# A recurrent scorer on one core: fp32 instructions of 50 rows for the item-0 correction, and a shorter setup

## Chip, cores and metric

One core of a Trainium2 chip. The metric is the device time of one execution in microseconds (us). Numbers of timed runs are medians of several executions. "Span" is the length of the profiled execution on the core, some 2 us less than the time of the same execution.

## The reference, cut to what matters

```python
emb = emb_table.at[0].set(0.0)              # item 0 counts as a row of zeros
e = emb[seq]                                # 1024 x 50 x 128
prefix = jnp.cumsum(e, axis=1)
uF = prefix / minimum(t + 1, lengths)       # running mean
y  = (uF - uF.mean(0)) * rsqrt(uF.var(0) + 1e-5) * gamma + beta
# scan over the 50 steps: v = v + (x - v)/2; spike = v >= 1; v = v - spike
scores = spikes.mean(over the steps) @ emb.T   # 1024 x 100001, fp32
```

The kernel gathers from the table as it lies in memory, where row 0 is not zero. So wherever the index is 0, row 0 has to be taken off again. That correction is what the change alters.

## The kernel before

Stage one runs through the 50 time steps. GpSimd gathers 1024 rows per step (eight gathers of 128 rows), TensorE transposes them into an accumulator `pre` in PSUM that runs through all steps, VectorE and ScalarE compute the running mean, the normalisation and the spikes, and TensorE counts the spikes. Stage two multiplies the counts with the table and writes 410 MB of scores.

```python
# gathers: three row buffers ("gather", bufs=3), tag "e"
def gather(t):
    es[t] = gp.tile([P, B], F32, tag="e")
    for n in range(NB):                      # NB = 8
        nc.gpsimd.indirect_dma_start(out=es[t][:, n*P:(n+1)*P], in_=table,
                                     in_offset=IndirectOffsetOnAxis(ap=idx[:, n, t:t+1]))
gather(0)
make_identity(nc, ident)
# ...
# the mask of zero indices, twice (rows 0..49 and 64..113), transposed to zT, 128 x 1024
isz = gp.tile([P, NB, P], F32, tag="e")
nc.vector.memset(isz, 0.0)
for u in (0, P // 2):
    nc.vector.tensor_single_scalar(isz[:, :, u:u+T], idx, 0.0, ALU.is_equal)
# ... eight transposes, then
nc.vector.tensor_copy(zT, zps)               # zT is float32r
# row 0 split into a rounded part (upper rows) and the rest (lower rows): r0n
rlen = once.tile([P, B], F32)
nc.vector.tensor_copy(rlen, len_i)           # 128 x 1024
nc.vector.reciprocal(rlen, rlen)             # 128 x 1024

def row0(t):                                 # ScalarE: row 0 into the rows t and 64 + t
    nc.scalar.activation(l, r0n, AF.Copy, scale=sel[:, t:t+1])
def correct(t, l):                           # TensorE: one float32r pass for each half of the batch
    for h in range(2):
        nc.tensor.matmul(pre[h], lhsT=l, rhs=zT[:, h*BANK:(h+1)*BANK], start=t == 0, stop=False)

# a time step t
gather(t + 1)                                # cut: the place of this call
# transposes of step t into pre[h]; uF = max(rlen, 1/(t+1)) * pre[h]; bn_stats
correct(t + 1, l)
# normalisation on VectorE and ScalarE; spikes; then
counted(t - 1, s, h)                         # TensorE, behind the correction
```

## Time and profile before

| | before |
|---|---|
| time, 3 runs | 1645.34 us (1644.9 to 1645.82) |
| profiled span | 1721.3 us |
| stage one, until the first output matmul | 593.4 us in the profile |
| gathers | 400 on GpSimd, 0.947 us each and 0.30 us between them |
| correction | 100 matmuls, 72.7 us in all |
| first uF | at 28.66 us |

How to read the profile. The busy tenths cut the span into 40 slices, one digit a slice. A group line gives engine, operation, tiles and number, then busy us, mean ns of one, and the engine's idle time ahead of it with what ended it. "issue" as a releaser is time in which the engine waited for nothing that the profile shows, and "remote" one for which it found no releaser. A timeline row is start, duration, engine, line, tiles, and in brackets the idle time before it. POOL is GpSimd, PE is TensorE, DVE is VectorE, ACT is ScalarE. The lines are in the prediction.

Note that the profiled execution took 1723.2 us, 78 us longer than the timed ones.

### The profile page before, as it was taken

The page shows a single profiled execution, that of the slowest core. Times are in us where ns is not written, and L with a number is a line of the kernel's source. Part 1 is how long each engine was busy: PE and PEld are TensorE (multiplying, and loading weights), DVE is VectorE, ACT ScalarE, POOL GpSimd, SP SyncE. Part 2 cuts the span into 40 slices and gives each one's busy share as a digit, 9 for nine tenths or more (in the row PEclk, how much of TensorE's full clock was granted, in tenths as well). Part 3 has the DMA queues.
Part 4 walks back from the last instruction along what each step waited for, and adds up shares of the span by engine and source line. Part 5 has one row for each costly group of instructions (what it writes and reads, how often), then busy time and mean ns, then how long its engine had stood idle before and what let it go on. Part 6 is the DMA issues. An engine that isn't in the chain of part 4 may idle for free.

```text
span 1721.3 us, 13874 instructions
## 1 busy us (share of the span) xinstructions
PE 1141.8 (66%) x4526; PEld 820.3 (48%) x4526; DVE 969.4 (56%) x1261; ACT 636.3 (37%) x698; POOL 379.5 (22%) x406
## 2 busy tenths in 40 slices
PE   2233333433344478877788777877778888888886
PEld 1112222221222356655566555666556666666664
DVE  5557756765667645554455444554445555555554
ACT  1222222221223344443444434444334444444443
POOL 7666666666666000000000000000000000000000
PEclk9855555555555599999999999998998899999999
DMA  9811111111111199999999999999999999999998
GB/s 267 234 44 48 48 48 44 48 49 46 45 49 46 38 391 397 401 400 393 388 394 402 394 391 393 395 400 390 396 396 390 403 410 414 402 405 406 403 402 349
DMA packets 98004, 488.75 MB, mean 284 GB/s; under 512 B 14827, under 2 KB 16652, under 8 KB 48780
## 3 DMA queue, kind: packets, MB, share of 16 engines
q1 hardware_dynamic: 85132, 461.63, 68.9%
q0 software_dynamic: 12800, 26.24, 5.3%
q8 instruction: 35, 0.57, 0.1%
q14 instruction: 37, 0.30, 0.0%
HBM read 78.21 MB, written 409.60 MB: 283 GB/s over the span
## 4 chain that ended last, share of the span: by engine, by line
DMA 48%; DVE 23%; PE 10%; another core or an unknown queue 9%; ACT 5%; issue 4%; POOL 0%; ACTq 0%; DVEq 0%; SPq 0%
DMA scores<-o 48%; PE po L301 9%; DVE bs L229 4%; ACT o L311 4%; DVE uF L228 4%; DVE v L267 3%; DVE s L199 3%; DVE negv L266 2%; DVE o L309 2%; ACT v L264 1%; DVE mv L233 1%; DVE a L257 1%; DVE r L255 1%; DVE q L254 0%
## 5 line engine op out<-in xcount | busy, mean ns | idle before, releaser
L301 PE MATMUL po<-hi,countR 128*128 128x512 f32 x1568 | 679.9, 434 | 179.5 <-ACT o L311 176.4
L309 DVE TENSOR_SCALAR o<-po 128x1024 f32<-128x1024 f32 x392 | 478.9, 1222 | 460.3 <-DMA scores<-o 428.3
L301 PE MATMUL po<-lo,countR 128*128 128x512 f32 x1568 | 645.0, 412 | 0.0
L311 ACT ACTIVATE o<-po 128x1024 f32<-128x1024 f32 (+1 forms) x392 | 399.9, 1020 | 633.2 <-DMA scores<-o 506.0
L301 PEld LDWEIGHTS po<-hi,countR 128*128 128x128 f32 x1568 | 316.0, 202 | 330.5 <-ACT o L311 243.0
L122 POOL DMA_INDIRECT e<-in_L_rec_emb_table,idx x400 | 378.8, 947 | 184.7 <-issue 109.3
L301 PEld LDWEIGHTS po<-lo,countR 128*128 128x128 f32 x1568 | 316.4, 202 | 60.1
L179 PE MATMUL pre<-zT,l 128*128 128x512 f32 x100 | 72.7, 729 | 264.4 <-DVE uF L228 196.0
L179 PEld LDWEIGHTS pre<-zT,l 128*128 128x128 f32 x100 | 27.0, 271 | 306.0 <-issue 192.2
L92 DVE TENSOR_TENSOR lo<-pt,hi 128x1024 fp32r<-128x1024 f32 x98 | 119.7, 1221 | 87.9 <-ACT hi L91 86.2
L228 DVE SCALAR_TENSOR_TENSOR uF<-rlen,pre 128x512 f32<-128x512 f32 x100 | 67.9, 679 | 144.8 <-remote 129.3
L237 ACT ACTIVATE r<-mv,eps 128x1 f32<-128x1 f32 x50 | 14.7, 295 | 351.4 <-DVE mv L233 307.2
L90 PE MATMUL pt<-ident,rows 128*128 128x128 f32 x782 | 108.4, 283 | 19.3 <-ACT o L311 12.0
L90 PEld LDWEIGHTS pt<-ident,rows 128*128 128x128 f32 x782 | 89.2, 144 | 52.4 <-ACT o L311 38.2
L189 PE MATMUL count<-s,ident_h 128*128 128x512 bf16 x100 | 50.7, 608 | 88.9 <-DVE s L199 67.8
L91 ACT CAST hi<-pt 128x1024 fp32r<-128x1024 f32 x98 | 98.5, 1005 | 16.1 <-remote 11.3
L219 PEld LDWEIGHTS pre<-ident,e 128*128 128x128 f32 x400 | 86.7, 228 | 21.3 <-issue 18.6
L219 PE MATMUL pre<-ident,e 128*128 128x128 f32 x400 | 95.4, 418 | 0.0
L264 ACT ACTIVATE v<-uF,hgb,a 128x1024 f32<-128x1024 f32 (+1 forms) x51 | 60.8, 1192 | 52.0 <-DVE r L255 16.2
L229 DVE BATCH_NORM_STATS2 bs<-uF 128x6 f32<-128x512 f32 x100 | 69.4, 694 | 3.4
L267 DVE SCALAR_TENSOR_TENSOR v<-negv,v 128x1024 f32<-128x1024 f32 (+1 forms) x51 | 61.6, 1209 | 15.6 <-issue 7.3
L189 PEld LDWEIGHTS <-ident_h 128*128 128x128 bf16 x100 | 12.2, 122 | 103.2 <-issue 102.9
(41 smaller groups left out, 286.3 us busy)
## 6 DMA issues: line engine op xcount, KB each, us to landing
scores<-o SPq DMA_DIRECT2D x384, 1024.0 KB
scores<-o SPq DMA_DIRECT2D x8, 848.5 KB
e<-in_L_rec_emb_table,idx POOLq DMA_INDIRECT x400
rows<-in_L_rec_emb_table SPq DMA_DIRECT2D x1, 832.0 KB
rows<-in_L_rec_emb_table SPq DMA_DIRECT2D x48, 0.5 KB
len_i<-in_r_lengths SPq DMA_DIRECT2D x1, 512.0 KB
idx<-in_r_seq SPq DMA_DIRECT2D x1, 200.0 KB
r<-in_L_rec_emb_table SPq DMA_DIRECT2D x1, 64.0 KB
```

The lines of the kernel that those rows point to most:

```text
L90: nc.tensor.transpose(pt[:, k0 : k0 + kw], r[:kw, (h0 + k0) // P, :], ident[:kw, :kw])
L91: nc.scalar.copy(hi[:, :hw], pt[:, :hw])
L92: nc.vector.tensor_tensor(lo[:, :hw], pt[:, :hw], hi[:, :hw].bitcast(F32), ALU.subtract)
L122: nc.gpsimd.indirect_dma_start(out=es[t][:, n * P : (n + 1) * P], out_offset=None, in_=table, in_offset=bass.IndirectOffsetOnAxis(ap=idx[: ...
L179: nc.tensor.matmul(pre[h], lhsT=l, rhs=zT[:, h * BANK : (h + 1) * BANK], start=t == 0, stop=False, skip_group_check=True,)
L219: nc.tensor.matmul(pre[h][:, k : k + P], lhsT=e[:, h * BANK + k : h * BANK + k + P], rhs=ident, start=False, stop=last, is_transpose=True, ...
L228: nc.vector.scalar_tensor_tensor(uF[:, cs], rlen[:, cs], 1.0 / (t + 1), pre[h], ALU.max, ALU.mult)
L229: nc.vector.bn_stats(bs[:, h, :], uF[:, cs])
L267: nc.vector.scalar_tensor_tensor(vt[:, cs], negv[:, cs], -0.5, vt[:, cs], ALU.mult, ALU.add)
L301: nc.tensor.matmul(po[:, k0 : k0 + kw], lhsT=countR[:, n * P : (n + 1) * P], rhs=part[:, k0 : k0 + kw], start=j == 0, stop=j == 1,)
L309: nc.vector.tensor_scalar_mul(o[:, h0 : h0 + hw], po[:, :hw], 1.0 / T)
L311: nc.scalar.mul(o[:, h0 : h0 + hw], po[:, :hw], 1.0 / T)
```

## The change

The intent is an exact and simpler correction: one true fp32 product of 50 rows (one per time step) in place of the split into two float32r parts in 100 of 128 rows; and a setup that takes reciprocals of 128x8 lengths instead of a 128x1024 broadcast. "Four instructions" in the short description are, as I read it, the four that the hardware profile records for a step: two for each of the two matmuls.

```diff
-        len_i = up.tile([P, B], I32, tag="uF", name="len_i")
-        nc.sync.dma_start(out=len_i, in_=lengths...to_broadcast([P, B]))
-        r0 = once.tile([P, D], F32, tag="r0", name="r0")
+        len_i = once.tile([P, NB], I32, tag="len_i", name="len_i")
+        nc.sync.dma_start(out=len_i, in_=lengths.rearrange("(n p) -> p n", p=P))
+        r0 = once.tile([T, D], F32, tag="r0", name="r0")
 ...
+        make_identity(nc, ident)
         gather(0)
-        make_identity(nc, ident)
 ...
-        isz = gp.tile([P, NB, P], F32, tag="e", name="isz")
-        nc.vector.memset(isz, 0.0)
-        for u in (0, P // 2):
-            nc.vector.tensor_single_scalar(isz[:, :, u : u + T], idx, 0.0, ALU.is_equal)
+        isz = gp.tile([P, NB, T], F32, tag="e", name="isz")
+        nc.vector.tensor_single_scalar(isz..., idx..., 0.0, ALU.is_equal)
 ...
-        zT = once.tile([P, B], F32R, tag="zT", name="zT")
-        nc.vector.tensor_copy(zT, zps)
-        (row 0 split in two parts, and the selector sel)
+        zT = once.tile([T, B], F32, tag="zT", name="zT")
+        nc.scalar.copy(zT, zps[:T, :])
+        r0n = once.tile([T, D], F32, tag="r0n", name="r0n")
+        nc.vector.tensor_scalar_mul(r0n, r0, -1.0)
+        rl = once.tile([P, NB], F32, tag="rl", name="rl")
+        nc.vector.tensor_copy(rl, len_i)
+        nc.vector.reciprocal(rl, rl)
+        rb = gp.tile([P, NB, P], F32, tag="e", name="rb")
+        nc.vector.tensor_copy(rb, rl.unsqueeze(2).to_broadcast([P, NB, P]))
+        (eight transposes of rb into rps)
-        nc.vector.tensor_copy(rlen, len_i)
-        nc.vector.reciprocal(rlen, rlen)
+        nc.vector.tensor_copy(rlen, rps)
 ...
-            l = sp.tile([P, D], F32R, tag="l", name=f"l_{t}")
-            nc.scalar.activation(l, r0n, AF.Copy, scale=sel[:, t : t + 1])
+            l = sp.tile([T, D], F32, tag="l", name=f"l_{t}")
+            nc.scalar.activation(l, r0n, AF.Copy, scale=ident[:T, t : t + 1])
```

More of the change, by code (lines that the diff above doesn't have):

```diff
@@ L44, in rec_kernel @@
     NB = B // P
-    assert D == P and B == HALF and T <= P // 2
+    assert D == P and B == HALF and T <= P
     ctx.enter_context(tc.manual_schedule())
@@ L106, in rec_kernel @@
         nc.sync.dma_start(out=idx, in_=seq.rearrange("(n p) t -> p n t", p=P))
-        len_i = up.tile([P, B], I32, tag="uF", name="len_i")
-        nc.sync.dma_start(out=len_i, in_=lengths.rearrange("(o b) -> o b", o=1).to_broadcast([P, B]))
-        r0 = once.tile([P, D], F32, tag="r0", name="r0")
-        nc.sync.dma_start(out=r0, in_=table[0:1, :].to_broadcast([P, D]))
+        len_i = once.tile([P, NB], I32, tag="len_i", name="len_i")
+        nc.sync.dma_start(out=len_i, in_=lengths.rearrange("(n p) -> p n", p=P))
+        r0 = once.tile([T, D], F32, tag="r0", name="r0")
+        nc.sync.dma_start(out=r0, in_=table[0:1, :].to_broadcast([T, D]))
         gb = once.tile([P, 2], F32, tag="gb", name="gb")
@@ L141, in rec_kernel @@
+        nc.vector.tensor_single_scalar(
+            isz.rearrange("p n t -> p (n t)"), idx.rearrange("p n t -> p (n t)"), 0.0, ALU.is_equal
+        )
         zps = vp.tile([P, B], F32, tag="v1", name="zps")
         for n in range(NB):
-            nc.tensor.transpose(zps[:, n * P : (n + 1) * P], isz[:, n, :], ident)
-        zT = once.tile([P, B], F32R, tag="zT", name="zT")
-        nc.vector.tensor_copy(zT, zps)
-        r0hi = once.tile([P, D], F32R, tag="r0hi", name="r0hi")
-        nc.scalar.copy(r0hi, r0)
@@ L148, in rec_kernel @@
-        r0n = once.tile([P, D], F32, tag="r0n", name="r0n")
-        nc.vector.tensor_scalar_mul(r0n, r0hi.bitcast(F32), -1.0)
-        up2 = slice(P // 2, P)
-        nc.vector.tensor_tensor(r0n[up2, :], r0hi[up2, :].bitcast(F32), r0[up2, :], ALU.subtract)
-        sel = once.tile([P, P // 2], F32, tag="sel", name="sel")
-        nc.vector.tensor_tensor(sel, ident[:, : P // 2], ident[:, P // 2 :], ALU.add)
+            nc.tensor.transpose(zps[:T, n * P : (n + 1) * P], isz[:, n, :], ident)
+        zT = once.tile([T, B], F32, tag="zT", name="zT")
@@ new lines, in rec_kernel @@
+        nc.scalar.copy(zT, zps[:T, :])
[6 more added lines that the diff above has]
+        nc.vector.tensor_copy(rb, rl.unsqueeze(2).to_broadcast([P, NB, P]))
+        rps = vp.tile([P, B], F32, tag="v0", name="rps")
+        for n in range(NB):
+            nc.tensor.transpose(rps[:, n * P : (n + 1) * P], rb[:, n, :], ident)
```

## The prediction

> **What bounds the kernel now.** I read the busy tenths first, to cut the run into stages, then the groups, the waits of GpSimd, and last the timeline of the start and of one step in the middle. Busy tenths in 40 slices of 43 us:
>
> ```profile
> POOL 7666666666666000000000000000000000000000
> PEclk9855555555555599999999999998998899999999
> DMA  9811111111111199999999999999999999999998
> ```
>
> There are two stages. In the first 13 to 14 slices GpSimd (POOL) gathers embedding rows, the DMA engines are nearly empty after the first two slices, and TensorE runs at half its clock. In the rest POOL is idle and DMA is full: the scores are written. The table by stretches puts the first output matmuls at 594.0 us, so the second stage is 1721.3 - 594.0 = 1127.3 us. The change touches nothing in it. Groups and the waits of POOL:
>
> ```profile
> L122 POOL DMA_INDIRECT e<-in_L_rec_emb_table,idx x400 | 378.8, 947 | 184.7 <-issue 109.3
> L179 PE MATMUL pre<-zT,l 128*128 128x512 f32 x100 | 72.7, 729 | 264.4 <-DVE uF L228 196.0
> ...
> POOL e L122 <- issue: 109.3, 358, 0.6
> POOL e L122 <- remote: 64.4, 16, 5.4
> ```
>
> A gather takes 0.947 us and 109.3/358 = 0.30 us pass before the next, so 1.25 us each; eight make a time step, so 10.0 us per step and 500 us for fifty. L179 is the group that the change alters. One step in the middle (start, duration, engine, line):
>
> ```profile
> 302.71 0.68 DVE L228 SCALAR_TENSOR_TENSOR uF<-rlen,pre 128x512 f32<-128x512 f32 x1
> 303.54 0.77 PE L179 MATMUL pre<-zT,l 128*128 128x512 f32 x1 [1.43 <-DVE uF L228]
> 304.76 0.80 PE L179 MATMUL pre<-zT,l 128*128 128x512 f32 x1 [0.46 <-DVE uF L228]
> 305.85 1.21 DVE L199 TENSOR_SCALAR s<-v 128x1024 bf16<-128x1024 f32 x1
> 307.12 1.01 PE L189 MATMUL count<-s,ident_h 128*128 128x512 bf16 x2 [1.55 <-DVE s L199]
> 307.92 1.91 PE L219 MATMUL pre<-ident,e 128*128 128x128 f32 x8
> 310.44 0.68 DVE L228 SCALAR_TENSOR_TENSOR uF<-rlen,pre 128x512 f32<-128x512 f32 x1
> ```
>
> When the rows are there, a step is 310.44 - 302.71 = 7.73 us, and VectorE works through nearly all of it. That is less than the 10.0 us of POOL. So stage one is **bound by the issue of the gathers**, and VectorE has 2.3 us per step to spare.
>
> One thing does not fit: POOL also waited 64.4 us in 16 waits marked "remote", about one in three steps, because the transposes that free a row buffer were late (TensorE's were recorded at 315.65, but VectorE could read the result at 321.64 and 330.04). I don't know the cause. But the profiled run has 1721.3 us and the timed ones 1645.3, 76 us less. Without these waits the last gather would end at 3.8 + 0.7 + 500 = 504.5 us; its data lands 1.3 us later by the packet records, the last step takes some 15 us (transposes at 578.0 to 594.0 in the profile), and the second stage 1127: in all 1648 us, an estimate within 0.2% of the timed 1645.3. So I take it that the timed runs are bound by POOL without interruption.
>
> The start:
>
> ```profile
> 3.81 1.09 POOL L122 DMA_INDIRECT e<-in_L_rec_emb_table,idx  x1 [3.36 <-DMA idx<-in_r_seq]
> ...
> 13.64 0.23 POOL masks.py:197 MEMSET ident<- 128x128 f32 x1
> 13.95 0.29 POOL masks.py:199 TENSOR_SCALAR_AFFINE_SELECT ident<-ident 128x128 f32<-128x128 f32 x1
> ...
> 14.40 0.96 POOL L122 DMA_INDIRECT e<-in_L_rec_emb_table,idx  x1 [0.16 <-issue]
> ...
> 21.10 6.55 DVE L158 RECIPROCAL rlen<-rlen 128x1024 f32<-128x1024 f32 x1
> ...
> 28.66 0.63 DVE L228 SCALAR_TENSOR_TENSOR uF<-rlen,pre 128x512 f32<-128x512 f32 x1
> ```
>
> POOL starts when the indices land and runs at its beat, apart from 0.75 us for the identity. VectorE's setup is long, but POOL doesn't wait for it.
>
> **What the Trainium skill says.** "FP8 and Floating Point Precision", section TensorE Precision Notes: true FP32 takes four passes through the array, a reduced FP32 read takes one. The kernel before has no true fp32 matmul (its transposes are another mode), so its trace can't confirm the four. "TensorE: Matmul & The Clock Gate", section Part 1: a cold array runs at 1.2 GHz, so 512 columns are 427 ns from start to start. The trace agrees roughly: PEclk is 5 tenths in stage one, and two bf16 matmuls of 512 columns take 1.01 us together where one alone takes about 0.6. The same page, section Why this matters for your kernels, says that a single matmul of K=32 takes as long as one of K=128: so 50 rows instead of 128 save nothing. "VectorE: DVE Perf Modes", section First, the fixed hardware budget: reciprocal is an iterative division; the trace has 6.55 us for it where the int-to-float cast of the same size took 0.85.
>
> **The change part by part.**
>
> Correction, per step. Before: two matmuls, 0.77 + 0.80 = 1.57 us. After: 2 x 4 passes. Back to back that is 8 x 0.43 + 0.35 (the 0.78 of one alone less 0.43) = 3.8 us, so 2.2 us more per step, 110 us more of TensorE in all. Where it lies: the first half may start at 303.54 as now, so the eight passes end at 307.35. The count behind it waits for the spikes until 305.85 + 1.21 = 307.06 anyway and starts at 307.12: it is put off by about 0.25 us. The next transposes then start at 308.2 and the first four of them are over at about 309.3, while VectorE takes them up at 310.44. So the passes fit even into the fast step, with 1.1 us to spare. If no weight load overlaps (0.27 us each in the group of L179's loads), the eight take 8 x 0.70 = 5.6 us, the first four transposes end at about 311.1, and the fast step becomes 8.4 us: still under 10.0. TensorE's total per step would be 5.6 + 1.0 + 1.9 = 8.5 us at worst. On the path that sets the end: 0 us.
>
> Operand of the correction (ScalarE): 50x128 instead of 128x128, same free size, so the same 0.39 us. 0 us.
>
> Setup on VectorE. Taken away: memset 0.91, one of two compares 0.33, the zT copy 1.23 (now on ScalarE), two small instructions 0.5, the cast 0.85 and the reciprocal 6.55: 10.4 us. Added: cast and reciprocal of 128x8 at 0.15 each (the 128x1 ones take 0.15), a broadcast copy of 128x1024 at about 0.9, a copy from PSUM at about 1.2, and on TensorE eight transposes of about 1.9 us: 2.4 us of VectorE. So the first uF comes some 8 to 9 us sooner, at 19 to 21 us instead of 28.66; not sooner, because the last rows of step 0 land at 18.5 by the packet records. But the rows of step 1 land only at 28.6, those of step 2 at 39.4: by step 1 or 2 the lead is used up in waiting for POOL. Worth on the path: 0 us.
>
> Identity before the first gather: POOL makes it while it waits for the indices, and the second group of gathers starts at about 13.95 instead of 14.40. Worth -0.5 us, all on the path.
>
> Row buffers. The setup now takes two of the three row buffers. The order of the built program shows that the gather of step 1 takes the one of the zero mask (it waits for VectorE and TensorE), that of step 2 the one of the spread reciprocals, that of step 3 the one of step 0. The first two are read by about 13 us: the gathers shouldn't wait. 0 us.
>
> Lengths: 1024 elements of 4 bytes instead of 128 rows of 4 KB. Needed by about 12 us; nothing on POOL hangs on it. 0 us.
>
> Sum: -0.5 us, with small risks all on the slow side. I put **1645.5 us**.
>
> **Rivals.** (1) TensorE becomes the bound of a step. It would need over 10 us per step, so over 7 us for eight passes; at 8 us each step would be 11 us and the total 1695. The 427 ns and even exposed weight loads speak against it. (2) The late transposes of the profile are there in timed runs too, and more passes make them later or more frequent: if each of the 16 waits grew by the added 2.2 us, +35 us, 1680. For it: nothing in the profile names their cause. Against it: the sum of 1648 without them. (3) The setup is on the path and its 8 us are gained: 1637. Against it: POOL never waits for VectorE at the start. (4) The second group of gathers waits for a buffer, until step 0 is transposed at about 19 us: +5 us, 1650. The order of the program speaks against it.
>
> **Range and chances.** Between (3) and (4) with run-to-run spread lies 1637 to 1650; I lean the range to the slow side for part of (2). Faster by over 2% means under 1612, for which I see no source: 0.02. Slower by over 2% means over 1678, which needs (1) or all of (2): 0.05.
>
> **What would show it.** In the changed kernel's profile POOL should keep 1.25 us per gather, with the second group at about 14 us; the first uF should come at 19 to 21 us and the second step still wait for rows; L179 should show some 1.9 to 2.8 us per half in place of 0.78, and the count should start within 0.5 us after the spikes; a fast step should stay between 7.7 and 8.5 us; the second stage should stay at 1127 us. I would be wrong if steps are over 10 us with no wait for rows, or if POOL's "remote" waits grow and the timed runs grow with them.

## The result

| same chip, same rounds | median | range | runs |
|---|---|---|---|
| before | 1645.55 us | 1644.9 to 1645.82 | 4 |
| changed | 1644.55 us | 1644.27 to 1646.15 | 4 |

The ratio is 0.9996, with a 95% interval of 0.9979 to 1.0014: the same time.

The profiled run of the changed kernel has a span of 1642.6 us, so this time it is like the timed ones. Its busy tenths, in slices of 41 us:

```profile
POOL 7777777777771000000000000000000000000000
PEclk6555555555556899999999999999999999999999
DMA  9921222221223999999999999999999999999998
```

GpSimd is at 7 tenths in every slice of stage one; before, it fell to 6. The first output is evicted at 517.2 us in place of 595.7. Groups of the changed kernel, and the first of GpSimd's waits:

```profile
L122 POOL DMA_INDIRECT e<-in_L_rec_emb_table,idx x400 | 377.7, 944 | 124.3 <-issue 115.5 <-DMA e<-in_L_rec_emb_table,idx 3.4 <-DMA idx<-in_r_seq 2.7
L179 PE MATMUL pre<-zT,l 50*128 50x512 f32 x200 | 186.8, 1086 | 2.3 <-DVE uF L228 2.3
...
POOL e L122 <- issue: 115.5, 379, 0.3
```

The gathers wait for nothing but their own beat (115.5 us in 379 gaps of 0.3). The 64.4 us of "remote" waits are gone (not through the change, as the experiments show; the kernel before has no profile of the shorter kind). The correction has grown from 72.7 to 186.8 us of recorded TensorE time, at double the number of records. A step in the middle, from the timeline of the changed kernel:

```profile
302.23 0.68 DVE L228 SCALAR_TENSOR_TENSOR uF<-rlen,pre 128x512 f32<-128x512 f32 x1
...
305.69 3.78 PE L179 MATMUL pre<-zT,l 50*128 50x512 f32 x4
...
307.62 1.21 DVE L199 TENSOR_SCALAR s<-v 128x1024 bf16<-128x1024 f32 x1
...
309.40 1.04 PE L189 MATMUL count<-s,ident_h 128*128 128x512 bf16 x2
...
310.23 1.06 PE L219 MATMUL pre<-ident,e 128*128 128x128 f32 x4
...
312.22 0.68 DVE L228 SCALAR_TENSOR_TENSOR uF<-rlen,pre 128x512 f32<-128x512 f32 x1
```

The step is 312.22 - 302.23 = 9.99 us, the beat of eight gathers. The correction takes 3.78 us for both halves, as the prediction's 8 x 0.43 + 0.35 had it. The count starts 309.40 - 308.83 = 0.57 us after the spikes end. The transposes that follow come in pieces, because they wait for rows.

The start of the changed kernel:

```profile
0.74 0.20 POOL masks.py:197 MEMSET ident<- 128x128 f32 x1 [0.29 <-POOLq L328]
...
4.05 1.10 POOL L122 DMA_INDIRECT e<-in_L_rec_emb_table,idx  x1 [2.74 <-DMA idx<-in_r_seq]
...
4.75 0.20 DVE L151 RECIPROCAL rl<-rl 128x8 f32<-128x8 f32 x1
...
14.30 0.94 POOL L122 DMA_INDIRECT e<-in_L_rec_emb_table,idx  x1 [0.30 <-PE pre L219]
15.26 0.69 DVE L228 SCALAR_TENSOR_TENSOR uF<-rlen,pre 128x512 f32<-128x512 f32 x1 [4.95 <-PE pre L219]
```

The reciprocal takes 0.20 us in place of 6.55. The first uF comes at 15.26 us, 13.4 us sooner than before, and nothing comes of it: the last gather ends at 503.4 us, where the beat of the gathers alone puts it (4.05 + 400 x 1.25 - 0.30 = 503.75). The identity is made at 0.74 us, while GpSimd waits for the indices.

### The profile page after: what moved, and what is told of

The parts are those of the page before. It is cut to its first block, busy times and chain, and to the rows that moved or that the text cites. A ratio compares the mean times of both kernels' runs of the same rounds, so it can differ in the third digit from the quotient of the medians.

```text
span 1642.6 us, 14074 instructions
## 1 busy us (share of the span) xinstructions
PE 1294.6 (79%) x4621; PEld 837.6 (51%) x4634; DVE 963.5 (59%) x1258; ACT 637.1 (39%) x698; POOL 378.4 (23%) x406
## 4 chain that ended last, share of the span: by engine, by line
DMA 54%; POOL 16%; PE 12%; issue 8%; DVE 5%; ACT 4%; DVEq 0%; ACTq 0%; SPq 0%; POOLq 0%
DMA scores<-o 51%; POOL e L122 16%; PE po L301 10%; ACT o L311 3%; DVE o L309 3%; DMA e<-in_L_rec_emb_table,idx 3%; PE pre L179 1%; PE pt L90 1%; PE pre L219 0%; DVE s L199 0%; DVE bs L229 0%; DVE uF L228 0%; ACT v L264 0%; DVE v L267 0%; PE count L189 0%
## 5 line engine op out<-in xcount | busy, mean ns | idle before, releaser
L122 POOL DMA_INDIRECT e<-in_L_rec_emb_table,idx x400 | 377.7, 944 | 124.3 <-issue 115.5
L219 PE MATMUL pre<-ident,e 128*128 128x128 f32 x400 | 143.0, 443 | 122.8 <-DMA e<-in_L_rec_emb_table,idx 118.7
L179 PE MATMUL pre<-zT,l 50*128 50x512 f32 x200 | 186.8, 1086 | 2.3 <-DVE uF L228 2.3
L219 PEld LDWEIGHTS pre<-ident,e 128*128 128x128 f32 x400 | 80.3, 206 | 202.1 <-DMA e<-in_L_rec_emb_table,idx 179.4
L179 PEld LDWEIGHTS pre<-zT,l 50*128 50x128 f32 x200 | 57.4, 317 | 65.3 <-issue 38.4
L199 DVE TENSOR_SCALAR s<-v 128x1024 bf16<-128x1024 f32 (+1 forms) x51 | 60.9, 1194 | 0.1
L266 DVE TENSOR_TENSOR negv<-s,v 128x1024 f32<-128x1024 bf16 x48 | 58.1, 1211 | 0.0
```

The lines of the kernel that those rows point to most:

```text
L122: nc.gpsimd.indirect_dma_start(out=es[t][:, n * P : (n + 1) * P], out_offset=None, in_=table, in_offset=bass.IndirectOffsetOnAxis(ap=idx[: ...
L179: nc.tensor.matmul(pre[h], lhsT=l, rhs=zT[:, h * BANK : (h + 1) * BANK], start=t == 0, stop=False, skip_group_check=True,)
L219: nc.tensor.matmul(pre[h][:, k : k + P], lhsT=e[:, h * BANK + k : h * BANK + k + P], rhs=ident, start=False, stop=last, is_transpose=True, ...
```

## The experiments

**The theory.** Stage one is bound by the issue of the gathers, so the passes (hidden by the slack of the step) and the setup (used up in waiting for rows) cost and gain nothing. **Rivals.** The passes do cost and the setup gains as much, so that the two cancel; or the late transposes of the profile of before are a property of the kernel that the change removed, and the timed runs hide it.

Twelve runs were made, on three chips that are named here by number: 14, 2 and 7. The chips of the first profile and of the first comparison are not on record.

| run | edit | chip | median, us | kernel before there | ratio, 95% interval |
|---|---|---|---|---|---|
| before_again | none | 2 | 1728.16 | 1729.01 | 0.9994 (0.9978 to 1.0009) |
| corr_only | correction alone | 2 | 1732.42 | 1729.01 | 1.0019 (1.0005 to 1.0033) |
| setup_only | setup alone | 2 | 1729.20 | 1729.01 | 1.0001 (0.9988 to 1.0015) |
| corr_x2 | changed, 16 passes | 2 | 1739.83 | 1729.01 | 1.0058 (1.0042 to 1.0073) |
| after_again | changed | 14 | 1645.42 | 1646.35 | 0.9996 (0.9983 to 1.001) |
| half_before | before, 4 gathers a step | 14 | 1558.70 | 1646.35 | 0.9469 (0.9454 to 0.9483) |
| half_corr | correction, 4 gathers | 14 | 1551.49 | 1646.35 | 0.9427 (0.9413 to 0.9442) |
| half_after | changed, 4 gathers | 14 | 1549.64 | 1646.35 | 0.9414 (0.9399 to 0.9428) |
| corr_x2b | changed, 16 passes | 14 | 1648.30 | 1646.39 | 1.0007 (0.9992 to 1.0023) |
| corr_x3 | changed, 24 passes | 14 | 1716.40 | 1646.39 | 1.0426 (1.0402 to 1.045) |
| ahead17 | changed, one more chunk fetched | 14 | 1642.70 | 1646.39 | 0.9979 (0.9967 to 0.9992) |
| after_third | changed | 7 | 1726.97 | 1726.52 | 1.0009 (0.9992 to 1.0025) |

The three with 4 gathers are wrong (relative error 0.77); all others are correct.

### before_again: is it the one profiled execution?

No edit.

> The kernel before, unchanged, profiled a second time. Theory A (the late transposes of the first profile belong to that one execution or to being profiled, not to the kernel's timed runs): time ratio to the kernel before 1.000 within 0.1%; if it was that one execution, the new profile has a span near 1643 us and no waits of POOL marked 'remote'; if it is this kernel under the profiler, the span is again near 1721 with some 64 us of such waits while the timed runs stay near 1645. Rival B (the waits are in the timed runs as well): a profile of 1721 us and timed runs that now and then show 1700 us or more.

On chip 2 all runs of the kernel before take 1727 to 1730 us, the profiled one and the others. Neither theory had that. The waits of GpSimd:

```profile
POOL e L122 <- PE pre L179: 38.9, 9, 4.4
POOL e L122 <- remote: 29.7, 7, 5.5
```

These are 38.9 + 29.7 = 68.6 us in 16 waits, one about every third step, as in the first profile of before. (L179 is the correction, which reads no row buffer; under both names GpSimd waits for TensorE to be done with the transposes that free one.) So, against theory A, **the late transposes do not belong to the one profiled execution**. Whether recording plays a part is not shown: every timed run carries a span and a clock too. The kernel has two times: some 1645 us on chip 14 and in the first comparison, some 1728 us on chips 2 and 7. Within one chip the runs agree within 0.15%. Chip 14 was used in two jobs, chips 2 and 7 in one each, so "chip" may also stand for the session; below, "kind of chip" is short for that. The mean granted clock doesn't tell the kinds apart (0.80 to 0.82 in the runs of before on chip 2, 0.79 to 0.93 in runs on chip 14). The first profile of before (1721.3) was of the longer kind; its timed runs were of the shorter.

### corr_only and setup_only: the two parts apart

```diff
 corr_only: from before
+ fp32 correction of 50 rows: isz, zT, r0n, row0() as in the change
 setup_only: from before
+ make_identity before gather(0); lengths 128x8; reciprocal 128x8, spread, eight transposes
```

> Only the correction changed to fp32 over 50 rows; setup and order of the kernel before. Theory (bound by the issue of the gathers, the passes lie in slack): 1645 us, within 1 us of the kernel before; in the profile the four fp32 instructions of a step take 3.8 us from first start to last end and POOL keeps 1.25 us per gather. Rival 1 (the passes are on the path): 2.2 us per step more, 110 us in all, 1755 us.

> Only the short setup and the identity ahead of the first gather; float32r correction as before. Theory: 1644 to 1645.5 us, that is 0 to 1 us less, all of it from the second group of gathers that starts at about 14.0 instead of 14.4 us. Rival 3 (the setup is on the path): 8 to 13 us less, 1632 to 1637 us.

On chip 2 the correction alone costs 3.4 us in the medians (0.19%, the interval leaves out a ratio of 1), more than the 1 us expected; the setup alone costs nothing. A cancellation of two large terms is ruled out there: neither is large. The setup brings the first uF from 28.8 to 15.4 us in its profile and the time doesn't move.

### after_again, after_third: the changed kernel on both kinds of chip

No edit.

> The changed kernel as it is, once more, because the last job ran the kernel before at 1729 us and not at 1645. If this job's kernel before takes about 1645: ratio 0.999 to 1.000 and no late transposes. If it takes about 1729: the two parts alone gave +3.4 us (fp32 passes) and 0 (setup) there, so if the parts add up 1730 to 1734 us, with some 65 to 75 us of waits of POOL for row buffers; if the changed kernel escapes the late transposes altogether, about 1645.

> The changed kernel a third time, in case this run falls on a chip where the kernel before takes about 1729 us instead of 1645, where only the two parts of the change have been run so far (1.0019 for the correction, 1.0001 for the setup). If it does: the late transposes stall the gathers in both kernels and the sum of the parts is 1.002, so about 1732 against 1729; rival (more passes make the transposes later, by my prediction's second rival, 2.2 us in each of 16 waits): 1765. If it falls on a chip of the other kind: 1645 against 1646, a ratio of 0.9996 as in the two runs before, which then adds only a third chip.

On chip 14 the ratio is 0.9996 again. On chip 7, where the kernel before takes 1726.52, the changed one takes 1726.97: the ratio is 1.0009. So the change leaves the time alone on both kinds; the sum of the parts on chip 2, 1.002, is not seen here. The waits of GpSimd in the changed kernel on chip 7, and the step in which they arise:

```profile
POOL e L122 <- remote: 60.8, 15, 4.4
```

```profile
318.68 1.92 PE L219 MATMUL pre<-ident,e 128*128 128x128 f32 x8
...
326.97 0.94 POOL L122 DMA_INDIRECT e<-in_L_rec_emb_table,idx  x1 [0.30 <-issue]
331.77 0.69 DVE L228 SCALAR_TENSOR_TENSOR uF<-rlen,pre 128x512 f32<-128x512 f32 x1 [10.61 <-remote]
332.14 0.94 POOL L122 DMA_INDIRECT e<-in_L_rec_emb_table,idx  x1 [4.22 <-remote]
```

The eight transposes are recorded at 318.68 to 320.60, as always (their ends are modelled). VectorE can read their result only at 331.77, 4.8 us after GpSimd issued its last gather at 326.97. GpSimd meanwhile lacks a free row buffer and stands for 4.22 us. Then two quick steps follow, and it begins anew: the steps of this profile go 7.7, 7.7, 18.4 us, which is 33.8 us for three or 11.3 us a step, in place of 10.0. The kernel before has the like on chip 2 (7.7, 17.0, 9.3, in all 34.0 us for three), and each has 16 such waits, of about 4 us apart from one of 7.0 on chip 7. The prediction's second rival, that added passes make each of these waits longer by 2.2 us, would have given some 35 us more: not so.

What makes the transposes late on some chips stays open. The packed trace of the step above narrows it. TensorE's completion events, nine for the count and the eight transposes, come at 322.65, 324.75, 327.54, 329.64 and 331.74 us, and the last four by 331.88: one in 2 to 3 us while gathers are being issued and landing, and quickly once they stop. The rows are not late: by the packet records the last packet of a gather is in SBUF 2.2 us after the gather's start (median) in both kinds, and the rows of this step are there by 319.3. Another sign tells the kinds apart: all six profiles of the longer kind kept only 1200 to 1811 of the gathers' 6400 landing events, the others all but a handful, so that their pages give no time from issue to landing where the others give 2.5 us. Whether this is a cause or a consequence is not shown. Nor does the array's clock in stage one tell the kinds apart, as far as its readings can be trusted (see the last section): the tables by stretch give 0.57 on the first profile of before, 0.55 on chip 7 and 0.50 in the changed kernel's first profile, which has no such waits. No experiment took the suspected contention between gathers and transposes away, since the chip could not be chosen.

### Half the gathers: is it the gathers that bind?

```diff
-            for n in range(NB):
+            for n in range(NB // 2):
 ...
-                        lhsT=e[:, h * BANK + k : h * BANK + k + P],
+                        lhsT=e[:, k : k + P],
```

Both halves of the batch then read the same 512 rows: the result is wrong, the work of all other engines the same.

> The kernel before with four gathers per step instead of eight (wrong result on purpose: the second half of the batch reuses the first half's rows). POOL needs 5.0 us per step, so VectorE's 7.73 us should set the step. Theory (gathers bind now): first uF at 28.7, 49 steps of 7.73 and four prepared tiles of 2.8 us more, 11 us to the output stage, 1127 us of output: 1558 us. If something else binds (a wait that is not the gathers'), 1620 us or more.

> Only the fp32 correction, with four gathers per step (wrong result on purpose). Theory (the passes fit into VectorE's step with about 1 us to spare): within 5 us of the half_before run. Rival (passes on the path as soon as the gathers are not): 30 to 110 us more than half_before.

> The changed kernel with four gathers per step (wrong result on purpose). Theory: the setup is on the path once POOL is not, so 10 to 13 us less than half_before, and the passes cost nothing. Rival (setup hidden behind the first rows even then): the same as half_corr.

The time of before falls by 1646.35 - 1558.70 = 87.7 us, to what was expected. GpSimd now waits for buffers, not for itself; the waits of half_before:

```profile
POOL e L122 <- PE pre L219: 153.6, 46, 7.3
POOL e L122 <- issue: 46.7, 153, 0.6
```

Steps are 7.7 us in all three, apart from those that prepare table tiles, so the eight fp32 passes cost nothing even in a step that VectorE bounds, as the prediction's "1.1 us to spare" has it (the passes are a little shorter here, 954 ns a record in place of 1086). And the shorter setup does count once gathers don't bind: half_after is 9.1 us faster than half_before, and its first uF comes at 15.4 us in place of 23.8. Most of it comes with the correction's own part of the setup (half_corr: 7.2 us, first uF at 18.2), which has no memset and leaves the copy of zT to ScalarE. Both missed what I had expected: half_corr within 5 us of half_before, half_after 10 to 13 us below it. One more number was off: I had expected the first uF of half_before where it stood in the full kernel, at 28.7, and it came at 23.8, because the identity is made behind four gathers and not eight (at 9.05 and not 13.95); the steps that prepare table tiles near the end were longer than I had put them (12.2 and 10.7 us), so that the total came out right with two errors against each other.

### More passes: how large is the reserve of TensorE?

```diff
-                nc.tensor.matmul(pre[h], lhsT=l, ...)
+                for j in range(2):      # corr_x2, corr_x2b; range(3) in corr_x3
+                    nc.tensor.matmul(pre[h], lhsT=l if j == 0 else zero_l, ...)
```

The added matmuls have zero weights, so the result stays right.

> The changed kernel with every correction matmul followed by one more with zero weights into the same sums (right result): 16 passes instead of 8 per step, 7.2 us instead of 3.8 by the 0.43 us from pass to pass. Theory: TensorE then needs 7.2 + 1.0 + 1.9 = 10.1 us per step against POOL's 10.0, so it is just at its limit: 1644 to 1665 us. Rival (passes on the path): plus 3.4 us per step, 170 us, 1815 us.

> 16 passes per step again, because the first run of it fell on a chip where the kernel before takes 1729 and not 1645. TensorE needs 16 x 0.43 + 0.35 + 1.0 + 1.9 = 10.1 us per step against POOL's 10.0, but three row buffers let POOL run ahead: on a chip where the kernel before takes 1645: 1645 to 1665, most likely 1650. Rival (passes are dearer than 0.43 us, or nothing of them is hidden): 49 x 3.4 = 170 us more, 1815. Where the kernel before takes 1729: as before, about 10 us over it.

> 24 fp32 passes per step in place of 8; the added sixteen have zero weights, so the result stays right. My step term says that TensorE then needs 24 x 0.43 + 0.35 + 1.0 (count) + 1.9 (transposes) = 13.6 us per step, more than POOL's 10.0: TensorE takes the bound of stage one, and the time grows by about 49 x (13.6 - 10.0) = 176 us less what the hidden start gives back, about 1800 to 1825 where the kernel before takes 1645. If the passes overlap with something that I count as serial (the transposes waiting, the count of the step before), less: 1720 to 1800. Rival (fp32 passes cost nothing on the path here, whatever their number, because something else sets the step): under 1660. Where the kernel before takes 1729 (about 11.3 us per step), 1800 to 1840.

Sixteen passes cost 10.8 us on chip 2 (0.58%). GpSimd's waits for row buffers are there

```profile
POOL e L122 <- remote: 72.9, 23, 5.8
POOL e L122 <- PE pre L223: 9.5, 5, 2.9
```

or 82.4 us in 28, against 68.6 in 16 in before_again: on this kind, added passes do make the waits more frequent. (One profile each: corr_only has 71.1 us in 19 and setup_only 70.1 in 16.) On chip 14 the same passes cost nothing that can be told from zero (1.9 us in the medians, the interval includes 1). So on the shorter kind twice the change's passes would still have been hidden. Twenty-four are too many: 70.0 us. GpSimd then waits for the transposes, 53.3 us in 28 waits:

```profile
POOL e L122 <- PE pre L223: 53.3, 28, 5.3
```

That a limit comes between 16 and 24 is as expected, but I had put its size at 155 to 180 us, or at least 75 if passes overlapped with something. Two timeline rows of corr_x3, four recorded matmuls each, in one and the same step, and the table by stretches (after the stretch and its length: busy us and number for PE, PE's loads, DVE, ACT, POOL; then the granted clock of TensorE):

```profile
308.71 1.88 PE L183 MATMUL pre<-zT,zero_l 50*128 50x512 f32 x4
311.78 3.61 PE L183 MATMUL pre<-zT,zero_l 50*128 50x512 f32 x4
```

```profile
307.50:310.00 2.50, 2.35 (x8) 1.04 (x6) 2.36 (x6) 0.04 (x1) 1.79 (x2) 1.00 0.12 26
312.50:315.00 2.50, 2.50 (x4) 0.66 (x2) 2.06 (x2) 1.33 (x2) 1.88 (x3) 0.50 0.22 56
```

The same four take 3.61 us at a granted clock of 0.50 and 1.88 us at 1.00. Steps wholly at the low clock are 13.3 us long in this profile, close to my 13.6; but in many steps TensorE has the full clock for a part, and those take 7.7 to 10.8 us. The mean from the second step to the last is (574.5 - 33.1) / 48 = 11.3 us. The step term of the sum had the right passes and a clock that holds for only a part of these steps. "TensorE: Matmul & The Clock Gate", section What's actually happening, in the Trainium skill, says that the default is throttled and activity releases the throttle. The traces agree only in part: 0.50 over stage one in the changed kernel's first profile and 0.64 with three times the passes, but 0.57 in the first profile of before, where TensorE is busy for half as long, and 0.93 in the changed kernel's second. What made the clock rise within these steps is not shown.

### ahead17: one more chunk fetched ahead, fewer buffers

```diff
-AHEAD = 16
+AHEAD = 17
-        gp = ph.enter_context(tc.tile_pool(name="gather", bufs=3))
-        up = ph.enter_context(tc.tile_pool(name="uF", bufs=2))
+        gp = ph.enter_context(tc.tile_pool(name="gather", bufs=2))
+        up = ph.enter_context(tc.tile_pool(name="uF", bufs=1))
```

> The changed kernel with 17 instead of 16 chunks of the table fetched before and during the first stage, paid for with two row buffers instead of three and one uF buffer instead of two. The output stage is bound by its transfers (about 397 GB/s in the profiles so far), and it then has one chunk of 1 MB less to read: 1.05 MB / 397 GB/s = 2.6 us less. Theory (stage one is bound by the issue of the gathers, and two row buffers are enough because a step's transposes are over long before the step after next starts to gather; stage two by the transfers): about 1642.5 where the kernel before takes 1645, and 2.6 us less too where it takes 1729, if the two buffers don't make the stalls there worse. Rival (the third row buffer hides the latency of the rows): POOL waits each step for the transposes, 1 us or more per step, 1690 or more. Rival (the fetches in stage two are hidden behind the writes): 1645, no gain.

It takes 1642.70 us, 3.7 us less than the kernel before in the medians (ratio 0.9979, the interval leaves out 1) and 2.7 us less than the changed kernel on the same chip, where 2.6 were expected. The gain is in stage two: the first output matmul starts at 515.0 us in its profile and at 515.1 in the changed kernel's second, and from there to the end it is 1125.9 us in place of 1128.1. So one megabyte less in stage two and two row buffers that are enough in stage one fit, on this kind of chip; the two edits were not run apart. On the other kind, where a missing row buffer is just what GpSimd waits for, it hasn't been run.

## Why the prediction was right

Going by its own steps:

- **The time**: 1645.5 predicted, 1644.55 measured. Right, and the ratio of 0.9996 repeats.
- **The bound** ("bound by the issue of the gathers"): shown by the half gathers, which take 88 us off, and by the profile, in which GpSimd has no wait beyond its usual 0.30 us once the indices are there.
- **The passes**: 3.8 us per step predicted, 3.78 measured; cost on the path 0, shown by 16 passes being free on chip 14 and by the 7.7 us steps with half the gathers. The delay of the count was put at 0.25 us in the working and under 0.5 in the signs to look for; it was 0.57, without effect.
- **The setup**: gain on the path 0, shown by setup_only and, the other way round, by half_after, where 9 us appear once the gathers don't bind. The first uF came at 15.26 us and not at 19 to 21: I had taken the landing of the last rows of step 0 for both halves, while the first half needs only the first four gathers. The second half came at 20.18, within what I said.
- **The identity**: the second group of gathers started at 14.30 and not 13.95 us, mostly because the indices landed later (first gather at 4.05 against 3.81). From the first gather to the second group it is 10.25 us in place of 10.59, a gain of 0.34. In the time, the -0.5 us of this term can't be told from the spread of the runs.
- **The late transposes**: this step was right for the runs it was made for and wrong as a reading. I wrote that I didn't know the cause and took it "that the timed runs are bound by POOL without interruption". On chips 2 and 7 the timed runs are interrupted. The sum of 1648 gave the right answer because the timed runs were on a chip of the shorter kind, which was luck; had they been on chip 7, the same change would have been measured at some 1727, far outside the range, with the same ratio. The sum itself is 5 us above the span of 1642.6: its end, from the last gather to the first output matmul, was read from the profile of the longer kind (1.3 + 15 us), and is 514.9 - 503.4 = 11.5 us. (There the first output matmul starts at 593.4 and not at 594.0, a slip without weight.)
- **Rival one** (TensorE becomes the bound) needed over 7 us for the passes: it comes true between 16 and 24 passes, not at 8. **Rival two** is answered by after_third: the late transposes are in both kernels, and with eight passes they don't grow (67.8 us in 16 waits on chip 7); with sixteen they do (82.4 in 28 on chip 2). **Rivals three and four** are answered by the profile: no setup gain, no wait of the second group beyond the usual 0.30 us gap.

What stays open is the cause of the late transposes, and with it whether the 0.19% of corr_only on chip 2 is theirs: its profile has 2.5 us more of these waits than before_again, but setup_only's has 1.5 us more at no cost in time.

## What to carry to other kernels

Before costing what a change adds to an engine, find the engine that sets the beat of that stage and count the slack of the others in one step: 2.2 us of added work in a step with more than 2.2 us of slack is worth nothing, and so is a setup shortened by 13 us if the first consumer then waits for data anyway. Halving the work of the supposed bound (with a wrong result) tests that claim in one run, and multiplying the added work finds where the slack ends. If a profile and the timed runs of one kernel differ by several per cent, run the unchanged kernel again on another chip before building a sum on either: the difference may belong to the chip or the session, and then only ratios taken there together mean anything.

## What the Trainium skill lacked or had wrong

- "FP8 and Floating Point Precision", section TensorE Precision Notes, gives true FP32 four passes. The runs agree: 3.78 us for eight passes of 512 columns, which fits 0.43 us from pass to pass and 0.35 at the end. It lacks that the profile records two instructions for each such matmul (200 records for 100), so that the count and the mean of 1086 ns aren't those of a matmul.
- "TensorE: Matmul & The Clock Gate", section Seeing it yourself, warns that recorded clock events can be unreliable. The runs agree: on chip 14 the tenths of the changed kernel's second profile show the clock at 9 in stage one, where its passes took as long as at 5 (1081 against 1086 ns per record):

```profile
PEclk9999999999756889889889999999999999999998
```

```profile
L179 PE MATMUL pre<-zT,l 50*128 50x512 f32 x200 | 186.4, 1081 | 2.8 <-DVE uF L228 2.4
```

- No page that I read gives the pace of row gathers on GpSimd: 0.944 us of it for 128 rows of 512 bytes and 0.30 us until the next, 1.25 us in all (944 to 947 ns in the full kernels' profiles).
- No page that I read has two times of one single-core kernel: 1645 us on one chip and 1727 to 1729 us on two others (chip or session, not separated), with TensorE's transposes late beside the gathers on the latter.
